# State space layer: the first sequence's halves of time in turn up to the softplus, gates and turned projections last

## The chip, the cores and the metric

One core of a Trainium2 chip runs the whole program. The metric is the device time of one execution in microseconds; for the kernel before it is the median of three runs. A trace of one further execution gives the start and end of every instruction on the engines: TensorE (PE, with PEld for its weight loads), VectorE (DVE), ScalarE (ACT), GpSimd (POOL), and the queues that issue transfers, SP's above all. Each engine works through its own queue in order.

## The reference, cut to what matters

The program is a network of eight layers on four sequences of 1024 steps with 128 features: attention, mixture of experts, gated attention, the mixture again, a state space layer, a gated feed-forward layer, a second attention and the feed-forward layer again. The change is inside the state space layer. Per sequence that layer computes:

```python
xn = (x - mu) / jnp.sqrt(var + EPS) * ln_gamma + ln_beta
xz = xn @ W_in.T
xs, z = jnp.split(xz, 2, axis=-1)            # 256 channels each
xc = conv over time of xs, 4 taps per channel, + conv_b
u = silu(xc)
proj = u @ W_xproj.T                          # 48 = 16 + 16 + 16 columns
dt_low, Bc, Cc = jnp.split(proj, [16, 32], axis=-1)
delta = softplus(dt_low @ W_dt.T + b_dt)
A = -jnp.exp(A_log)
for every step of time:                       # 16 states per channel
    h = exp(delta * A) * h + (delta * u) * B
    y = sum over states of h * C
y = (y + u * D) * silu(z)
return resid + y @ W_out.T
```

## The kernel before, in words

Channels lie on the partitions in two groups of 128 (g = 0, 1), time lies along the row in two halves of 512 (`HALVES`). The layer has two parts per sequence, both in `StateSpace.run`.

`prepare(b)` is a generator that makes what the scan of sequence b needs, a little with each step (`yield`). For b > 0 it first runs `turned_in(b)`: two normalisations (lines 1132 to 1150, statistics on VectorE, the scaling on ScalarE) and a transposition into `xt`. Then, in this order: the convolution as four matmuls per group and half with the taps folded into the input weights (line 1197), each followed by Silu into `u` (1203); the gates silu(z), one matmul (1210) and Silu into `gate` (1214) per group and half; the projection `proj`, two matmuls (1220) and a copy by ScalarE (1223) per half; the store of B's rows to device memory through SP's queue (`b_rows`, 1226); eight small transposes of `proj` (1229) and a copy (1231) into `by_time`, which holds C by time; then `delta` per group and half, one matmul (1239) and a `softplus`; last `du` = delta times u on VectorE (1247).

`softplus` (1100 to 1114) is max(x, 0) + log1p(exp(-|x|)), with log1p as a polynomial in factored form: on ScalarE Abs, Relu, Exp and four Squares, on VectorE four products of a chain (1113) and a last one into `delta` (1114). Its temporaries have one buffer each.

`scan(b, meanwhile)` loops over the 16 states n. Per state it reads row n of `b_rows` on all partitions (`bs`, SP's queue, 1254); per group ScalarE makes `decay` = exp(delta a) (1258), and VectorE makes the input `st` = du bs (1260) and scans along time in place (1261). Then TensorE turns the states (1267), ScalarE multiplies them with C into `hc` (1273), and TensorE adds them up in PSUM with an identity matmul (1274). Twice per state the scan takes one step of `meanwhile`, the preparation of the next sequence. After the 16 states the output is turned back (1289), u D is added (1293), the gate is multiplied (1296), and the output projection (1302) is added to the residual (1307).

The first sequence's preparation runs before any scan:

```python
for _ in prepare(0):
    pass
for b in range(B):
    scan(b, prepare(b + 1) if b + 1 < B else iter(()))
```

The pool `psum()` gives the preparation two PSUM buffers; `st` has four buffers, `decay` and `bs` two, `hc` three. The order of the instructions in an engine's queue is not quite that of the program: a scheduler places each by the buffers and inputs that it needs, so that instructions of the preparation and of the scan stand interleaved. It also puts a load of a function table in front of an activation whose function isn't in the table that ScalarE holds: Silu, Exp and Sqrt are in different ones; Abs, Relu, Copy, Identity and Square get by with any. The gather of the mixture layer before (line 796) ends just ahead of the first Silu, which waits for it because `u` takes memory that the mixture held.

Of the kernel before, what the change touches and what calls it, by code (L numbers as in the profile page):

```python
# [11 lines left out]
F32 = mybir.dt.float32  # L12
# [8 lines left out]
P = 128  # L21
B = 4
T = 1024
C = 128
NC = T // P
# [12 lines left out]
D_STATE = 16  # L38
D_CONV = 4
DT_RANK = 16  # L40
# [136 lines left out]
class Start:  # L177
# [8 lines left out]
    def steps(self, bank, pin):  # L186
        self.bank, self.pin = bank, pin
        while self.open:
            if next(self.gen) is False:
                self.open = False  # L190
            yield
# [863 lines left out]
class StateSpace(Begun):  # L1055
# [60 lines left out]
    def run(self, start):  # L1116
        k, tc, nc, NG = self.k, self.k.tc, self.k.nc, self.NG
        per = self.per
        PAD = D_CONV - 1
        NPROJ = DT_RANK + 2 * D_STATE  # L1120
        with ExitStack() as ctx:
            early = ctx.enter_context(tc.tile_pool(name="s_early", bufs=1))
            yield
            HALVES = [slice(0, 512), slice(512, 1024)]
# [3 lines left out]
            roots = early.tile([P, len(LOG1P[1])], F32, name="roots")  # L1128
# [23 lines left out]
            def turned_in(b):  # L1152

                xl = early.tile([P, NC, C], F32, tag="xl", name="xl")
                yield from normal(xl, k.xb(b))
                nc.vector.tensor_tensor(k.xb(b), k.xb(b), xl, ALU.add)
                xn = early.tile([P, NC, C], F32, tag="xn", name="xn")
                yield from normal(xn, xl)
                for h in range(2):
                    ps = start.bank()  # L1160
                    for c in range(4):
                        start.pin(nc.tensor.transpose(ps[:, c * P : (c + 1) * P], xn[:, h * 4 + c, :], k.ident))
                    nc.scalar.activation(
                        xt[:, PAD + h * 512 : PAD + (h + 1) * 512], ps, AF.Identity,
                        scale=self.ln[:, 0:1], bias=self.ln[:, 1:2],
                    )
                    yield
# [6 lines left out]
            one = ctx.enter_context(tc.tile_pool(name="s_one", bufs=1))  # L1174
            sb = ctx.enter_context(tc.tile_pool(name="s_sb", bufs=2))
            dram = ctx.enter_context(tc.tile_pool(name="s_dram", bufs=2, space=DRAM))
# [3 lines left out]
            ready = {}  # L1180

            def psum():
                return ps_t.tile([P, 512], F32, tag="pt", name="ps")
# [3 lines left out]
            def prepare(b):  # L1187

                if b:
                    yield from turned_in(b)  # L1190
                u = sb.tile([P, NG, T], F32, tag="u", name="u")
                gate = sb.tile([P, NG, T], F32, tag="gate", name="gate")
                for g in range(NG):
                    for h in range(2):
                        ps = psum()
                        for t in range(D_CONV):
                            nc.tensor.matmul(  # L1197
                                ps, taps[:, t, g * P : (g + 1) * P], xt[:, h * 512 + t : h * 512 + t + 512],
                                start=t == 0, stop=t == PAD,
                            )  # L1200
                            if t == 1:
                                yield
                        nc.scalar.activation(
                            u[:, g, HALVES[h]], ps, AF.Silu, bias=per[:, g, D_CONV : D_CONV + 1]
                        )
                        yield
                for g in range(NG):
                    for half in HALVES:
                        ps = psum()
                        nc.tensor.matmul(  # L1210
                            ps, self.w_in[:, (NG + g) * P : (NG + g + 1) * P],
                            xt[:, PAD + half.start : PAD + half.stop], start=True, stop=True,
                        )
                        nc.scalar.activation(gate[:, g, half], ps, AF.Silu)
                    yield
                proj = one.tile([NPROJ, T], F32, tag="proj", name="proj")
                for half in HALVES:
                    ps = psum()
                    for g in range(NG):
                        nc.tensor.matmul(  # L1220
                            ps[:NPROJ], self.w_x[:, g, :], u[:, g, half], start=g == 0, stop=g == NG - 1
                        )
                    nc.scalar.copy(proj[:, half], ps[:NPROJ])
                    yield
                b_rows = dram.tile([D_STATE, T], F32, tag="b_rows", name="b_rows")
                nc.sync.dma_start(b_rows, proj[DT_RANK : DT_RANK + D_STATE, :])
                ps = psum()[:, : NC * NPROJ].rearrange("p (c n) -> p c n", c=NC)
                for c in range(NC):
                    nc.tensor.transpose(ps[:, c, :], proj[:, c * P : (c + 1) * P], k.ident[:NPROJ, :NPROJ])
                by_time = sb.tile([P, NC, D_STATE], F32, tag="by_time", name="by_time")  # L1230
                nc.scalar.copy(by_time, ps[:, :, DT_RANK + D_STATE :])
                delta = sb.tile([P, NG, T], F32, tag="delta", name="delta")
                du = one.tile([P, NG, T], F32, tag="du", name="du")
                ready[b] = gate, u, b_rows, by_time, delta, du
                yield
                for g in range(NG):
                    for half in HALVES:
                        ps = psum()
                        nc.tensor.matmul(
                            ps, self.w_dt[:, g * P : (g + 1) * P], proj[:DT_RANK, half], start=True, stop=True  # L1240
                        )
                        yield from self.softplus(
                            delta[:, g, half], ps, per[:, g, D_CONV + 1 : D_CONV + 2], early, roots
                        )
                        yield
                for g in range(NG):
                    nc.vector.tensor_tensor(du[:, g, :], delta[:, g, :], u[:, g, :], ALU.mult)

# [60 lines left out]
# [4 lines that stand above are left out]
# [568 lines left out]
```

## Time and profile before

| what | value |
|---|---|
| median of three runs | 3334.68 us (3333.33 to 3335.18) |
| the profiled execution, its own time | 3334.47 us |
| its span, first to last instruction | 3332.7 us |
| busy: TensorE, VectorE, ScalarE | 2974.0, 2326.5, 1820.5 us |
| VectorE's scans (1261): count, mean | 128, 2.28 us |
| hc copies (1273): count, mean | 512, 0.48 us |
| table loads in the carrying scans (from 1892.5 to 2345): mean | 1.28 us |
| VectorE's waits in scan 0, 1 and 2 | 13.1, 18.6 and 19.7 us |

A line of a time line gives start, duration, engine, line and operation, output and inputs with their shapes, the count, and in brackets the idle time of the engine before it with what ended it. TensorE runs an f32 matmul in two passes, and the trace lists each pass: x8 are four matmuls. A line of the table by stage gives the stretch, its length, the busy time and count of instructions of each engine, the granted clock of TensorE as a share of full speed, and the transfers' share and rate. Consecutive lines of a stretch of a time line overlap slightly, since an engine begins the next instruction before the last has quite ended.

### The profile page before, as it was taken

Reading aid. Unit: us, or ns where it says so; the run is one execution under the profiler, and the core shown is the slowest. Engines: PE = TensorE matmul, PEld = TensorE weight load, DVE = VectorE, ACT = ScalarE, POOL = GpSimd, SP = SyncE. Lnnn points to the kernel's source line nnn. Section 1 sums busy time; section 2 is a strip of 40 time slices with the busy share of each in tenths; the row PEclk is TensorE's granted clock in tenths of the full one; section 3 lists DMA queues with packets and bytes.
Section 4 is the critical chain, followed back from the end, with each engine's and each line's share of the span. In section 5 each row is a group of like instructions: output and inputs, shape, how many; then the busy total and the mean of one; then the engine's idle time right before and its main releaser. Section 6 shows DMA issues by size and latency. Waiting matters only on the chain. (4 is left out here: it accounts for less than half of the span.)

```text
span 3332.7 us, 46103 instructions
## 1 busy us (share of the span) xinstructions
PE 2974.0 (89%) x16624; PEld 1699.2 (51%) x16624; DVE 2326.5 (70%) x5413; ACT 1820.5 (55%) x3822; POOL 289.4 (9%) x299
## 2 busy tenths in 40 slices
PE   7999999999999988699897597888778899999988
PEld 4555555555555566445565244444445444444435
DVE  5777777777777667575564589888976767676634
ACT  4555555556555432355332698989653365555662
POOL 3000000000000014410034000000002101010000
PEclk9999999999999999799899798999999799898999
DMA  3110000000000001100011111111202111121100
GB/s 108 43 34 15 16 17 15 17 16 15 17 16 15 15 15 39 54 0 0 1 35 45 43 58 57 58 51 55 66 26 57 29 42 50 31 50 30 31 2 26
DMA packets 84901, 109.39 MB, mean 33 GB/s; under 512 B 26048, under 2 KB 66544, under 8 KB 82240
## 3 DMA queue, kind: packets, MB, share of 16 engines
q1 hardware_dynamic: 59136, 69.50, 6.7%
q0 software_dynamic: 18688, 30.65, 3.6%
q10 hardware_dynamic: 6848, 6.29, 0.6%
q8 instruction: 130, 2.13, 0.3%
q14 instruction: 99, 0.81, 0.1%
HBM read 90.76 MB, written 15.60 MB: 32 GB/s over the span
## 5 line engine op out<-in xcount | busy, mean ns | idle before, releaser
L389 ACT ACTIVATE p<-p,tops 128x640 f32<-128x640 f32 (+7 forms) x512 | 392.2, 768 | 288.0 <-DVE tops L387 226.6
L380 DVE CUSTOM_DVE_ANT_0 p<-s,mask 128x512 f32<-128x512 f32 (+3 forms) x768 | 392.0, 551 | 130.2 <-PE s L374 129.4
L1632 ACT ACTIVATE p<-x 128x512 f32<-128x512 f32 (+3 forms) x768 | 337.6, 490 | 249.1 <-PE x L1631 179.5
L1571 DVE TENSOR_REDUCE tops<-s 128x2 f32<-128x1024 f32 (+3 forms) x384 | 361.2, 955 | 137.0 <-PE s L1567 96.5
L1274 PE MATMUL acc<-hc,ident 128*128 128x512 f32 x512 | 270.2, 652 | 92.4 <-ACT hc L1273 91.6
L374 PE MATMUL s<-kt,qt 64*128 64x512 f32 (+3 forms) x1536 | 311.3, 516 | 20.2 <-DVE tops L380 19.8
L482 PEld LDWEIGHTS t<-ident,p 128*128 128x128 f32 x2304 | 263.0, 141 | 80.8 <-issue 66.3
L1261 DVE TENSOR_TENSOR_SCAN st<-decay,st 128x1024 f32<-128x1024 f32 x128 | 288.8, 2278 | 10.9 <-ACT decay L1258 10.4
L497 PE MATMUL o<-pt,vv 128*64 128x256 f32 (+1 forms) x2560 | 291.1, 365 | 0.0
L482 PE MATMUL t<-ident,p 128*128 128x128 f32 x2304 | 283.7, 273 | 1.6 <-ACT p L389 1.6
L1626 PE MATMUL x<-q,k 75*128 75x512 bf16 (+3 forms) x768 | 224.0, 339 | 27.5 <-ACT p L1632 14.9
L1562 PE MATMUL s<-k,q 72*128 72x512 bf16 (+3 forms) x768 | 217.0, 349 | 27.5 <-DVE tops L1571 19.2
L488 ACT COPY pt<-t 128x512 f32<-128x512 f32 (+1 forms) x320 | 155.2, 495 | 156.9 <-DVE pt L490 148.8
L1273 ACT ACTIVATE hc<-ps,by_time 128x256 f32<-128x256 f32 x512 | 200.6, 478 | 47.6 <-PE ps L1267 47.5
L490 DVE COPY pt<-t 128x512 f32<-128x512 f32 x320 | 212.2, 684 | 16.5 <-PE t L482 16.3
L497 PEld LDWEIGHTS o<-pt,vv 128*64 128x64 f32 x2560 | 166.8, 136 | 96.7 <-issue 28.5
L374 PEld LDWEIGHTS s<-kt,qt 64*128 64x128 f32 x1536 | 124.5, 187 | 146.1 <-issue 77.9
L1274 PEld LDWEIGHTS acc<-hc,ident 128*128 128x128 f32 x512 | 91.7, 198 | 208.5 <-ACT hc L1273 190.0
L1260 DVE TENSOR_TENSOR st<-du,bs 128x1024 f32<-128x1024 f32 x128 | 151.8, 1216 | 47.0 <-PE ps L1267 46.8
L696 PE MATMUL acc<-d,xl 128*128 128x480 f32 (+1 forms) x384 | 155.5, 567 | 27.7 <-DVE d L691 27.7
L1267 PEld LDWEIGHTS ps<-ident,st 128*128 128x128 f32 x1024 | 126.3, 147 | 97.0 <-issue 61.3
L1660 PE MATMUL o<-p,vx 128*32 128x512 f32 (+3 forms) x1536 | 173.7, 525 | 0.0
(301 smaller groups left out, 4778.9 us busy)
## 6 DMA issues: line engine op xcount, KB each, us to landing
bs<-b_rows SPq DMA_DIRECT2D x64, 512.0 KB
share<-shares SPq DMA_DIRECT2D x256, 64.0 KB
k<-b_parts POOLq DMA_DIRECT2D x16, 576.0 KB, 12.5
q<-b_parts POOLq DMA_DIRECT2D x48, 192.0 KB, 11.8
shares<-rows SPq DMA_DIRECT2D x512, 0.5 KB
b_parts<-part SPq DMA_DIRECT2D x24, 256.0 KB
w_W<-in_W_dram ACTq DMA_DIRECT2D x16, 256.0 KB
y_rows<-y SPq DMA_DIRECT2D x16, 192.0 KB
```

What stands on the lines that cost most here:

```text
L374: pe(nc.tensor.matmul(s[:, h, : hi - lo], q[feats, ib * P : (ib + 1) * P], kk[feats, lo:hi], start=True, stop=True,))
L380: ve(nc.vector.tensor_tensor_reduce(p[:, h, i, lo:hi], s[:, h, : hi - lo], m, -1.0, 3.4e38, ALU.add, ALU.min, tops[:, h, i, at : at + 1],))
L389: exp = nc.scalar.activation(p[:, h, i, :width], p[:, h, i, :width], AF.Exp, bias=tops[:, h, i, 0:1], scale=-1.0, accum_out=sums[:, h, i : ...
L482: pe(nc.tensor.transpose(t[:, m, h, i * P : (i + 1) * P], p[:, h, i, jb * P : (jb + 1) * P], k.ident))
L490: nc.vector.tensor_copy(pt[:, :, lo:], t[:, m, :, lo:])
L497: pe(nc.tensor.matmul(o[feats, lo:], pairs[n]["v"][:, jb, feats], pt[:, h, lo:], start=jb == 0, stop=jb == (gq + 1) * Q - 1,))
L1261: nc.vector.tensor_tensor_scan(st, decay, st, 0.0, ALU.mult, ALU.add)
L1274: nc.tensor.matmul(acc[:, c : c + 2, :].rearrange("p c d -> p (c d)"), k.ident, hc.rearrange("p c d -> p (c d)"), start=n == 0, stop=n == ...
L1562: start.pin(nc.tensor.matmul(s[:, a, : hi - lo], qq[:ROWS, two + a, ib * P : (ib + 1) * P], kk[:ROWS, two + a, lo:hi], start=True, stop=ha ...
L1571: nc.vector.tensor_reduce(tops[:, half, two : two + 2, n], s[:, :, : hi - lo], AX.X, ALU.max)
L1626: start.pin(nc.tensor.matmul(x[:, lo:], kk[:FULL, a, jb * P : (jb + 1) * P], qq[:FULL, a, hq * 512 + lo : (hq + 1) * 512], start=True, sto ...
L1632: nc.scalar.activation(p[:, a, lo:], x[:, lo:], AF.Exp)
```

## The change

`prepare` gets two inner generators. `products(h)` makes both groups of `u` for one half of time and the projection of that half; `steps(h)` makes `delta` of one half. For the first sequence the order is products(0), steps(0), products(1), steps(1): the first half goes through softplus before the second half is begun. For the others it is products(0), products(1), steps(0), steps(1). In both, `b_rows` is stored behind products(1); the turned projections (`by_time`) and the gates come behind the last softplus, `du` after them. What is computed is the same, and so is the number of steps that `prepare` yields.

```diff
--- before.py
+++ after.py
@@ -1190,8 +1190,12 @@
                     yield from turned_in(b)
                 u = sb.tile([P, NG, T], F32, tag="u", name="u")
                 gate = sb.tile([P, NG, T], F32, tag="gate", name="gate")
-                for g in range(NG):
-                    for h in range(2):
+                proj = one.tile([NPROJ, T], F32, tag="proj", name="proj")
+                delta = sb.tile([P, NG, T], F32, tag="delta", name="delta")
+
+                def products(h):
+
+                    for g in range(NG):
                         ps = psum()
                         for t in range(D_CONV):
                             nc.tensor.matmul(
@@ -1204,6 +1208,44 @@
                             u[:, g, HALVES[h]], ps, AF.Silu, bias=per[:, g, D_CONV : D_CONV + 1]
                         )
                         yield
+                    ps = psum()
+                    for g in range(NG):
+                        nc.tensor.matmul(
+                            ps[:NPROJ], self.w_x[:, g, :], u[:, g, HALVES[h]], start=g == 0, stop=g == NG - 1
+                        )
+                    nc.scalar.copy(proj[:, HALVES[h]], ps[:NPROJ])
+                    yield
+
+                def steps(h):
+
+                    for g in range(NG):
+                        ps = psum()
+                        nc.tensor.matmul(
+                            ps, self.w_dt[:, g * P : (g + 1) * P], proj[:DT_RANK, HALVES[h]], start=True, stop=True
+                        )
+                        yield from self.softplus(
+                            delta[:, g, HALVES[h]], ps, per[:, g, D_CONV + 1 : D_CONV + 2], early, roots
+                        )
+                        yield
+
+                yield from products(0)
+
+                if b == 0:
+                    yield from steps(0)
+                yield from products(1)
+                b_rows = dram.tile([D_STATE, T], F32, tag="b_rows", name="b_rows")
+                nc.sync.dma_start(b_rows, proj[DT_RANK : DT_RANK + D_STATE, :])
+                if b:
+                    yield from steps(0)
+                yield from steps(1)
+                ps = psum()[:, : NC * NPROJ].rearrange("p (c n) -> p c n", c=NC)
+                for c in range(NC):
+                    nc.tensor.transpose(ps[:, c, :], proj[:, c * P : (c + 1) * P], k.ident[:NPROJ, :NPROJ])
+                by_time = sb.tile([P, NC, D_STATE], F32, tag="by_time", name="by_time")
+                nc.scalar.copy(by_time, ps[:, :, DT_RANK + D_STATE :])
+                du = one.tile([P, NG, T], F32, tag="du", name="du")
+                ready[b] = gate, u, b_rows, by_time, delta, du
+                yield
                 for g in range(NG):
                     for half in HALVES:
                         ps = psum()
@@ -1213,36 +1255,6 @@
                         )
                         nc.scalar.activation(gate[:, g, half], ps, AF.Silu)
                     yield
-                proj = one.tile([NPROJ, T], F32, tag="proj", name="proj")
-                for half in HALVES:
-                    ps = psum()
-                    for g in range(NG):
-                        nc.tensor.matmul(
-                            ps[:NPROJ], self.w_x[:, g, :], u[:, g, half], start=g == 0, stop=g == NG - 1
-                        )
-                    nc.scalar.copy(proj[:, half], ps[:NPROJ])
-                    yield
-                b_rows = dram.tile([D_STATE, T], F32, tag="b_rows", name="b_rows")
-                nc.sync.dma_start(b_rows, proj[DT_RANK : DT_RANK + D_STATE, :])
-                ps = psum()[:, : NC * NPROJ].rearrange("p (c n) -> p c n", c=NC)
-                for c in range(NC):
-                    nc.tensor.transpose(ps[:, c, :], proj[:, c * P : (c + 1) * P], k.ident[:NPROJ, :NPROJ])
-                by_time = sb.tile([P, NC, D_STATE], F32, tag="by_time", name="by_time")
-                nc.scalar.copy(by_time, ps[:, :, DT_RANK + D_STATE :])
-                delta = sb.tile([P, NG, T], F32, tag="delta", name="delta")
-                du = one.tile([P, NG, T], F32, tag="du", name="du")
-                ready[b] = gate, u, b_rows, by_time, delta, du
-                yield
-                for g in range(NG):
-                    for half in HALVES:
-                        ps = psum()
-                        nc.tensor.matmul(
-                            ps, self.w_dt[:, g * P : (g + 1) * P], proj[:DT_RANK, half], start=True, stop=True
-                        )
-                        yield from self.softplus(
-                            delta[:, g, half], ps, per[:, g, D_CONV + 1 : D_CONV + 2], early, roots
-                        )
-                        yield
                 for g in range(NG):
                     nc.vector.tensor_tensor(du[:, g, :], delta[:, g, :], u[:, g, :], ALU.mult)
```

## The prediction

> **What bounds the kernel now.** First the busy time of each engine by stage: the fill (the first sequence's preparation, nothing beside it) and the four scans, the first three of which carry the next sequence's preparation.
>
> ```profile
> core 0: us, PE busy (x) PEld busy (x) DVE busy (x) ACT busy (x) POOL busy (x), PEclk, DMA share, GB/s
> 1839.70:1892.50 52.80, 23.03 (x50) 8.37 (x51) 24.44 (x31) 33.59 (x53) 0.00 (x0) 0.66 0.09 32
> 1892.50:2041.20 148.70, 126.53 (x470) 67.15 (x470) 134.89 (x130) 133.68 (x239) 0.00 (x0) 0.94 0.18 61
> 2041.20:2193.40 152.20, 127.50 (x504) 71.10 (x504) 134.18 (x135) 132.48 (x237) 0.00 (x0) 0.96 0.17 56
> 2193.40:2345.00 151.60, 127.99 (x485) 69.50 (x486) 129.88 (x142) 129.63 (x224) 0.00 (x0) 0.93 0.16 53
> ```
>
> In the fill no engine is full: it is a chain. In the scans three engines are near 90%, so the mean says little; what counts is where VectorE waits. Then the order of time in the fill:
>
> ```profile
> 1839.70 1.28 ACT L1203 ACT_TABLE_LOAD   x1 [25.11 <-DVE x L796]
> ...
> 1841.73 9.14 PE L1197 MATMUL ps<-xt,w_taps 128*128 128x512 f32 x16 [18.20 <-ACT u L1203]
> ...
> 1860.36 0.69 ACT L1106 ACTIVATE tmp<-ps,w_channels 128x512 f32<-128x512 f32 x1 [0.78 <-PE ps L1239]
> ...
> 1861.64 1.28 ACT L1108 ACT_TABLE_LOAD   x1
> ...
> 1862.94 0.63 ACT L1108 ACTIVATE tmp<-tmp 128x512 f32<-128x512 f32 x1
> ...
> 1868.14 2.07 PE L1239 MATMUL ps<-proj,w_wdtT 16*128 16x512 f32 x2 [5.34 <-ACT delta L1107]
> ...
> 1890.16 4.46 DVE L1261 TENSOR_TENSOR_SCAN st<-decay,st 128x1024 f32<-128x1024 f32 x2
> ```
>
> The start (1839.70) is set by the mixture's gather and can't move. ScalarE then waits for TensorE until 1860.36; its work until then is the first two u by 1842.3, two more (1.4), four gates (2.4), two proj copies (1.2), by_time (0.3): of 18.1 us it idles 12.9. The four softplus run after that, and the second channel group's first scan ends at 1892.4. The fill has two table loads (Silu, then Exp).
>
> Last, VectorE's waits. Those over 2 us that fall between the last u activation and the end of the first softplus's scans:
>
> ```profile
> 1960.98 1.23 DVE L1260 TENSOR_TENSOR st<-du,bs 128x1024 f32<-128x1024 f32 x1 [3.71 <-PE ps L1267]
> ```
> ```profile
> 2103.78 2.36 DVE L1260 TENSOR_TENSOR st<-du,bs 128x1024 f32<-128x1024 f32 x2 [3.37 <-PE ps L1267]
> ...
> 2112.40 1.23 DVE L1260 TENSOR_TENSOR st<-du,bs 128x1024 f32<-128x1024 f32 x1 [4.06 <-PE ps L1267]
> ```
> ```profile
> 2256.97 1.22 DVE L1260 TENSOR_TENSOR st<-du,bs 128x1024 f32<-128x1024 f32 x1 [4.62 <-PE ps L1267]
> ...
> 2264.81 1.23 DVE L1260 TENSOR_TENSOR st<-du,bs 128x1024 f32<-128x1024 f32 x1 [3.31 <-PE ps L1267]
> ...
> 2271.96 6.66 DVE L1261 TENSOR_TENSOR_SCAN st<-decay,st 128x1024 f32<-128x1024 f32 x3 [2.42 <-ACT decay L1258]
> ```
>
> A product st waits for a state buffer that TensorE's transposes free, and these wait for ScalarE. What ScalarE does then is seen in its own time line (scan 0):
>
> ```profile
> 1955.04 1.28 ACT L1214 ACT_TABLE_LOAD   x1
> 1956.33 1.09 ACT L1214 ACTIVATE gate<-ps 128x512 f32<-128x512 f32 x2
> ...
> 1959.38 1.28 ACT L1258 ACT_TABLE_LOAD   x1
> ```
>
> So each carrying scan has two halves. Up to softplus, ScalarE (u, gates and their table loads) and TensorE (taps, gates, proj) set the pace and VectorE waits; from softplus on, VectorE (6.7 us a state, from two products at 1.13 and two scans at 2.2, plus 3.5 to 3.8 a softplus block) sets it and waits for almost nothing (at most 1.1 us in one place) until the scan's end.
>
> **Part 1, the fill.** No arithmetic is added or removed; the order is, and with it the table loads. In the built order of instructions ScalarE's loads in the fill go from 2 to 10: the scheduler puts Silu (u, gates) between the Exp of the softplus blocks. Eight more at 1.28 us (row L1108) are 10.3 us, against 12.9 of idle time that may be filled. I walk ScalarE's queue in its built order, with steps from the fill's rows: u 0.65, Abs 0.6, Relu 0.7, Exp 0.7, square 0.7, gate 0.6, load 1.28; a TensorE pass (two to a matmul) 0.85 with the clock at half, 0.43 at full, its result 1.2 or 0.6 after the last start.
> - Two u end at 1842.3 as before. proj (four slow passes from 1841.73) is ready at 1845.4, copied by 1846.0; dt (2.07, row L1239) gives Abs at 1848.1.
> - Abs, Relu, load, Exp, three squares: 1853.65. Load, u, fourth square: 1856.2.
> - Abs, Relu, load, Exp, load, u: 1861.5.
> - Two squares, proj copy, two squares: 1864.7.
> - Abs, Relu, load, Exp, by_time, two squares, load, gate, two squares, gate: 1873.2.
> - The fourth block with two loads and two gates: 1881.6. VectorE then has a product, delta (1883.1), du (1884.3), the first scan, which now stands behind this (1886.6), two products (1888.8), the second group's scan: 1891.0.
>
> That is 1.4 before the old 1892.4. But before, ScalarE's normalising (L1147) and VectorE's statistics stood partly in gaps of the fill; now they follow. The third state's products start at 1899.9 instead of 1900.5: -0.6. This has TensorE at full clock after dt. At half clock, the second tap group is 2.1 late for its u, proj 1.0, dt and a gate 0.9 each: +4.9, so +4.3. The page "TensorE: Matmul & The Clock Gate" (Part 1) lets the clock fall only after an idle window of about 3.4 us; the new gaps are up to 3.2, so by it the term is -0.6. The trace differs: the granted clock was 1.00 in 1861 to 1862, 0.93 in the next microsecond and 0.50 in 1863 to 1864, right behind the last pass at 1862.8. I go by the row, half-way: **+1.5**, ends -0.6 and +4.3.
>
> A rule against the change: "ScalarE: Activation LUTs" (What ACT_TABLE_LOAD costs) adds a drain of 1.38 to each load, 2.66 a switch. The rows show none: Relu ends at 1861.6, the load starts at 1861.64, Exp at 1862.94. By the page the fill is 8 x 1.38 = 11.0 worse and four further loads in the scans up to 5.5: the sum below would be about +7. I take the row.
>
> The b_rows store now waits for the second proj copy (1863.4, was 1858.8) and SP's bs reads behind it: with the old 2.1 to the first issue and 5 us in which the trace moves both, they land by 1870.6; the first product needs them at 1873.7. Cover 3 us, cost nothing.
>
> **Part 2, the three carrying scans.** The scan takes two steps of the preparation a state. Softplus stood behind 13 steps (8 taps, 2 gates, 2 proj, 1), now behind 10: 1.5 states sooner, and the gates come last. I walk the queues of the three engines in their built order, with the scan's rows (hc copies of half a state 1.43, decay 1.05, a softplus's seven activations 4.2), from the end of the hc copies behind the fourth u (1950.5 in scan 0, 2101.4 in scan 1, 2254.7 in scan 2):
> - Old order, scan 0: gates, loads and proj follow. VectorE's next six scans (states 8 to 10) end 26.5 later (1976.9), with waits of 3.7 and 0.3 on the way.
> - New order: load, decay, proj copy, hc, decay, Abs, Relu, Exp, hc, squares. The same scans end at 28.0, but six softplus products and one delta (4.9) stand among them, work that the old order still had ahead. From there on VectorE sets the pace in both. Gain 4.9 - 1.5 = 3.4.
> - In front of this point TensorE has two proj matmuls more (1.7 us; TensorE 97% busy here): scan 0 keeps **-1.7**.
> - Scan 1: same walk, 27.3 against 26.5 with 3.4 done, and the old waits of 1.1 and 0.2 at the first softplus go too: 3.9, less 0.9 for the part of proj that a smoother row of taps doesn't absorb: **-3.0**.
> - Scan 2: the old order piled gates, proj, by_time and dt into one stretch (waits 4.6, 3.3, 2.4, 1.9); scans that ended at 2287.2 end at 2283.0 with 3.4 of softplus done: 7.6, less 1.1: **-6.5**.
>
> The gates themselves cost 4 loads and 4 activations, 7.3 to 7.5 us of ScalarE a scan (2 loads more than before in scans 0 and 1, none in scan 2: the 4 above). Their cover is VectorE. Walked from the decay of state 12: ScalarE has decay 26 ready at 14.7, VectorE asks at 17.2; decay 28 at 23.5, asked at 23.8; one state buffer 0.4 late. So they are hidden, but with 0.3 us to spare at the last. Behind a late decay would stand VectorE's scan, and behind it du and the next sequence's products. The b_rows store of the next sequence moves two places up SP's queue of bs reads in scan 0 (between those of states 9 and 10), one in the others; it waits for a copy at state 6 or 7, so no read queues behind it for long. xt is read by the gates until late, and is written again only in the next scan. Everything after the last scan is in the same order on all queues.
>
> **Sum.** +1.5 - 1.7 - 3.0 - 6.5 = **-9.7** on the profiled execution's 3334.47 (span 3332.7, 1.8 around it): 3324.8; the median of the runs is 0.2 above that: **3325**. A measurement of this kernel can't tell less than about 0.2%, 6.7 us, from nothing.
>
> **The rivals.**
> - A, the waits vanish altogether: all of VectorE's waits behind the fourth u (4.3, 8.8, 12.3: 25.4) and a fill at -0.6: 3309. For it: VectorE is full from there on. Against it: proj is now in the crowded half.
> - B, waits only move: proj and dt in front take what the gates gave, scans give nothing, fill +1.5: 3336. For it: ScalarE and TensorE are both above 96% in that half, and the same 8 loads for u remain.
> - C, slower: the gates' loads are not covered. VectorE's queue has four softplus products and a delta in a row just there; if ScalarE isn't ahead, each scan pays up to 7.3 us: +21.9 - 9.7, 3347. It decides from 5.5 us a scan on (slower by 6.7). For it: the reserve of 0.3. Against it: ScalarE idles for VectorE's squares now (8.4 us over the three scans).
>
> **How the numbers follow.** The forecast 0.54 (its own range 3318 to 3332, the clock's two ends and 3 us of error in the walks), A 0.10, B 0.19, C 0.17. 3328.0 and 3341.4 are the bounds. Faster: A, and four fifths of the forecast: 0.54. Same: the rest of it, most of B: 0.27. Slower: C with a tail of B: 0.19. The range leaves out a third of A and C's worse half: 3312 to 3343.
>
> **What would show it.** Right: 10 loads in the fill, scan's second-group start near 1891 to 1895, each softplus's first product two states sooner, carrying scans of 147, 149 and 145 us, no VectorE wait over 2 us behind the fourth u. Wrong: a fill over 57 us; VectorE waits on decay at states 13 and 14 beside gate loads; a gap behind each load; a scan no shorter although softplus came sooner.

## The result, and the profile after

The changed kernel takes 3347.5 us (median of 5 runs, 3344.6 to 3354.4) where the kernel before takes 3334.7 (5 runs beside it, 3331.4 to 3336.8): a ratio of 1.0046, 95% interval 1.0035 to 1.0058. It is slower, by 12.8 us; the forecast was 3325, and the range ended at 3343. The profiled execution took 3347.5 us, its span is 3345.8.

First the busy time by stage, of the kernel after, with the same columns as before (stretch, its length, busy time and count of instructions of each engine, granted clock of TensorE, transfers):

```profile
core 0: us, PE busy (x) PEld busy (x) DVE busy (x) ACT busy (x) POOL busy (x), PEclk, DMA share, GB/s
1839.70:1892.50 52.80, 29.57 (x56) 9.99 (x56) 26.02 (x30) 44.58 (x64) 0.00 (x0) 0.66 0.09 32
1892.50:2048.00 155.50, 128.01 (x466) 66.33 (x466) 134.70 (x135) 136.44 (x240) 0.00 (x0) 0.94 0.17 58
2048.00:2209.60 161.60, 134.48 (x504) 71.14 (x504) 134.63 (x134) 135.55 (x236) 0.00 (x0) 0.93 0.16 53
2209.60:2362.00 152.40, 127.85 (x482) 68.25 (x482) 128.63 (x137) 127.81 (x219) 0.00 (x0) 0.93 0.16 53
```

ScalarE is busier in the fill by 11.0 us, about the eight further loads. The first two carrying scans took 155.5 and 161.6 us, 6.8 and 9.4 more than before, while VectorE's busy time is within 0.5 us of what it was (134.9 and 134.2); the third took 152.4, 0.8 more. So VectorE waits, and the question is where.

**The measure used from here on.** The layer begins with the first u activation and ends, for this purpose, at the first line of VectorE that adds u D for the last sequence (1293 before, 1305 after). In the profiled execution of before that stretch is 1840.99 to 2473.54, 632.6 us; of after 1841.15 to 2491.44, 650.3: +17.7. What lies outside it is the same program in both, 2700.2 and 2695.5 us; in the executions profiled below it was 2690 to 2716, with no pattern that follows the edits. The stretch is therefore the sharper instrument of the two, and each experiment is given with both. It is taken from one execution of each kernel. How well it repeats is seen in its last part, in which nothing is carried: from the end of the third scan to that line of VectorE it took 136.7 to 138.3 us in all kernels but after_st6 and late_silu, whose edits reach into it. So differences of 1 or 2 us are not read as effects.

Within a scan I add up the idle times in brackets on VectorE's lines, from the scan's begin (in scan 0, from the first scan line of the second channel group) to the end of state 10's second scan ("front": u, proj and the first softplus fall here), and from there to the first scan line of the next sequence ("rear": the other softplus blocks, and in the kernel after the gates). The seams differ a little from those of the table ahead of the prediction; the sum for before is the same within 0.1.

| VectorE's waits, us | front: scan 0, 1, 2 | sum | rear: scan 0, 1, 2 | sum |
|---|---|---|---|---|
| before | 13.1, 16.1, 20.9 | 50.2 | 0.0, 1.3, 0.0 | 1.3 |
| after | 10.6, 15.7, 13.0 | 39.3 | 9.2, 10.6, 10.0 | 29.8 |

The front gained 10.9, where the forecast's three terms make 11.2. The rear, which the forecast gave nothing, lost 28.5. The difference, +17.6, is the stretch's +17.7 almost by itself. (Two of the expectations below have 30.1 for the rear of after: that takes in a wait of 0.27 us at the first line that adds u D.) Here is the rear of scan 0 in the time line of VectorE, kernel after:

```profile
2002.06 0.69 DVE L1114 SCALAR_TENSOR_TENSOR delta<-tmp,delta 128x512 f32<-128x512 f32 x1
2004.76 1.22 DVE L1272 TENSOR_TENSOR st<-du,bs 128x1024 f32<-128x1024 f32 x1 [2.00 <-PE ps L1279]
2005.90 2.28 DVE L1273 TENSOR_TENSOR_SCAN st<-decay,st 128x1024 f32<-128x1024 f32 x1
2008.10 1.20 DVE L1272 TENSOR_TENSOR st<-du,bs 128x1024 f32<-128x1024 f32 x1
2009.22 2.28 DVE L1273 TENSOR_TENSOR_SCAN st<-decay,st 128x1024 f32<-128x1024 f32 x1
2018.40 1.22 DVE L1272 TENSOR_TENSOR st<-du,bs 128x1024 f32<-128x1024 f32 x1 [6.91 <-PE ps L1279]
2019.55 2.28 DVE L1273 TENSOR_TENSOR_SCAN st<-decay,st 128x1024 f32<-128x1024 f32 x1
```

Read it by states. The two scans (1273) at 2005.90 and 2009.22 are those of state 13. The products (1272) at 2004.76 and 2008.10 belong to state **14**: the scheduler has set each in front of a scan of the state before. With four state buffers the next product, at 2018.40, the first of state 15, takes the buffer of state 13's first group. TensorE turns the two groups of a state in alternation, so this buffer is free only when nearly all of state 13 has been turned, and the second group was scanned an instruction ago. The product waits 6.91 us for it. TensorE shows the chain in that time (one line is one group; x8 are eight transposes):

```profile
2011.55 0.87 PE L1279 MATMUL ps<-ident,st 128*128 128x128 f32 x6 [2.81 <-DVE st L1273]
2013.09 3.78 PE L1286 MATMUL acc<-hc,ident 128*128 128x512 f32 x4 [0.66 <-ACT hc L1285]
2016.67 1.91 PE L1279 MATMUL ps<-ident,st 128*128 128x128 f32 x8
```

It had waited 2.81 for that very scan; then come transposes, the hc copies (ScalarE, 2012.20), the sum, the last transposes, and at 2018.4 the buffer is free. And ScalarE, in the same stretch, has the gates and their loads:

```profile
2008.11 1.28 ACT L1256 ACT_TABLE_LOAD   x1
2009.40 0.60 ACT L1256 ACTIVATE gate<-ps 128x512 f32<-128x512 f32 x1
2012.20 1.57 ACT L1285 ACTIVATE hc<-ps,by_time 128x256 f32<-128x256 f32 x4 [2.20 <-PE ps L1279]
2013.64 0.61 ACT L1256 ACTIVATE gate<-ps 128x512 f32<-128x512 f32 x1
2014.27 1.28 ACT L1270 ACT_TABLE_LOAD   x1
```

In before, VectorE's line at the same states has softplus work between almost any two steps, and no wait. The product of state 14 stands behind both scans of state 13, and that of state 15 (the last line here) comes 11 us after them:

```profile
2001.53 2.29 DVE L1261 TENSOR_TENSOR_SCAN st<-decay,st 128x1024 f32<-128x1024 f32 x1
2003.74 1.46 DVE L1113 SCALAR_TENSOR_TENSOR tmp<-tmp 128x512 f32<-128x512 f32 x2
2005.12 1.22 DVE L1260 TENSOR_TENSOR st<-du,bs 128x1024 f32<-128x1024 f32 x1
2006.25 0.69 DVE L1113 SCALAR_TENSOR_TENSOR tmp<-tmp 128x512 f32<-128x512 f32 x1
2006.86 2.28 DVE L1261 TENSOR_TENSOR_SCAN st<-decay,st 128x1024 f32<-128x1024 f32 x1
...
2013.58 1.46 DVE L1113 SCALAR_TENSOR_TENSOR tmp<-tmp 128x512 f32<-128x512 f32 x2
2014.95 1.22 DVE L1260 TENSOR_TENSOR st<-du,bs 128x1024 f32<-128x1024 f32 x1
```

In after, the same wait stands at 2180.39 in scan 1 (6.76) and at 2340.46 in scan 2 (6.07).

### The profile page after: what moved, and what is told of

Its sections match the earlier page's. It is cut to its first block, busy times and chain, and to the rows that moved or that the text cites. A ratio compares the mean times of both kernels' runs of the same rounds, so it can differ in the third digit from the quotient of the medians.

```text
span 3345.8 us, 46082 instructions
## 1 busy us (share of the span) xinstructions
PE 2985.0 (89%) x16624; PEld 1698.3 (51%) x16624; DVE 2328.6 (70%) x5413; ACT 1836.9 (55%) x3834; POOL 289.7 (9%) x299
## 5 line engine op out<-in xcount | busy, mean ns | idle before, releaser
L1574 PE MATMUL s<-k,q 72*128 72x512 bf16 (+3 forms) x768 | 217.9, 350 | 24.8 <-DVE tops L1583 17.2
L490 DVE COPY pt<-t 128x512 f32<-128x512 f32 x320 | 212.2, 684 | 17.2 <-PE t L482 17.1
L1279 PE MATMUL ps<-ident,st 128*128 128x128 f32 x1024 | 145.8, 285 | 41.6 <-DVE st L1273 41.6
```

The lines of the kernel that those rows point to most:

```text
L1279: nc.tensor.transpose(ps[:, m, g * P : (g + 1) * P], states[g][:, (c + m) * P : (c + m + 1) * P], k.ident,)
L1574: start.pin(nc.tensor.matmul(s[:, a, : hi - lo], qq[:ROWS, two + a, ib * P : (ib + 1) * P], kk[:ROWS, two + a, lo:hi], start=True, stop=ha ...
```

## The experiments

Two theories. **LOADS**: the gates' four loads and activations (7.3 us a scan) make decays and hc copies late, whatever VectorE's order is. **ORDER**: it is VectorE's queue, which the scheduler has built with a state's products in front of the scans of the state before.

### Which part: the fill or the scans

The kernel fill_only has the new order in the first sequence and the old one in the others:

```diff
+                if b == 0:
                     proj = one.tile([NPROJ, T], F32, tag="proj", name="proj")
...
+                else:
+                    for g in range(NG):
+                        for h in range(2):
+                            ps = psum()
+                            for t in range(D_CONV):
...
```

> The first sequence in the new order, the other three prepared in the old one; nothing is left out. Both theories of the loss (below) put it into the three carrying scans, so here only the fill's gain of 1.2 us is left: 3333 to 3334, VectorE's waits in the scans as before (13, 19, 20 us). If the fill's ten table loads cost something that the start of the scan hides, it is over 3336.

Measured: 3333.9 us, ratio 1.0001 (0.9991 to 1.0011); stretch 632.4, waits front 48.9, rear 3.0. The fill neither brings nor costs anything that can be measured; the loss is in the later sequences.

### The loads away, or the order away

gates_noload leaves the function out of the later sequences' gates, so that no load goes with them:

```diff
-                        nc.scalar.activation(gate[:, g, half], ps, AF.Silu)
+                        nc.scalar.activation(gate[:, g, half], ps, AF.Identity if b else AF.Silu)
```

> The changed kernel with the gates of sequences 1 to 3 computed by Identity in place of Silu, which leaves the Silu of the gates out of the result and needs no table; everything else is the same, in the same place. Table loads in the carrying scans go from 15, 15 and 16 to 11, 11 and 13. LOADS: 3329 to 3333 (4 loads, 5.1 us, a scan). ORDER: the built queue of VectorE loses the products in front of the scans too, so 3328 to 3336; this run bounds what the loads and what hangs on them cost, and doesn't part the two.

after_pinned keeps the gates and their loads, and ties VectorE's order: the first product of a state is placed behind the last scan of the state before, in the queue only, with no semaphore.

```diff
+                        product = nc.vector.tensor_tensor(st, du[:, g, :], bs, ALU.mult)
+                        if scanned is not None and g == 0:
+                            tc.add_manual_dep(
+                                product.ins, scanned.ins.name,
+                                mybir.DependencyInfo(mybir.DependencyClass.NoSync, mybir.DependencyReason.DATA),
+                                reason="order",
+                            )
+                        scanned = nc.vector.tensor_tensor_scan(st, decay, st, 0.0, ALU.mult, ALU.add)
```

> The changed kernel with one order added on VectorE's queue and no wait: the first product of a state stands behind the last scan of the state before. Theory ORDER (the loss is that VectorE's queue puts a state's products in front of the scans of the state before, so that behind softplus a product waits for the transposes of what was scanned just now): the waits of 6.9 and 6.8 us go, 3330 to 3337. Theory LOADS (the gates' four table loads and four activations, 7.3 us of ScalarE a scan, hold up decays and hc copies whatever VectorE's order): 3344 to 3350, with waits on decay in place of those on transposes.

Measured: gates_noload 3328.4, ratio 0.9985 (0.9974 to 0.9996), stretch 629.0; after_pinned 3327.2, ratio 0.9987 (0.9978 to 0.9996), stretch 632.1. Each alone takes the loss away. The first doesn't tell the theories apart, since without the loads the scheduler no longer sets products ahead at the end of scan 0; both products of state 14 stand behind the last scan of state 13:

```profile
2006.14 2.28 DVE L1273 TENSOR_TENSOR_SCAN st<-decay,st 128x1024 f32<-128x1024 f32 x1
2008.34 2.34 DVE L1272 TENSOR_TENSOR st<-du,bs 128x1024 f32<-128x1024 f32 x2
```

The second does: all of the gates' loads are there, and 18.2 us are gone, 10.6 of them in the rear. (The program is faster than ORDER's 3330 to 3337 had it, since the front lost 9.1 us of waits too, which neither theory had.) VectorE in the same place, after_pinned, and ScalarE's loads and decays beside it:

```profile
1997.78 0.69 DVE L1114 SCALAR_TENSOR_TENSOR delta<-tmp,delta 128x512 f32<-128x512 f32 x1
2001.34 2.29 DVE L1280 TENSOR_TENSOR_SCAN st<-decay,st 128x1024 f32<-128x1024 f32 x1 [2.87 <-ACT decay L1271]
2003.83 2.29 DVE L1280 TENSOR_TENSOR_SCAN st<-decay,st 128x1024 f32<-128x1024 f32 x1 [0.20 <-ACT decay L1271]
2006.04 2.33 DVE L1273 TENSOR_TENSOR st<-du,bs 128x1024 f32<-128x1024 f32 x2
2011.37 2.29 DVE L1280 TENSOR_TENSOR_SCAN st<-decay,st 128x1024 f32<-128x1024 f32 x1 [3.00 <-ACT decay L1271]
```
```profile
1998.87 1.28 ACT L1271 ACT_TABLE_LOAD   x1
2000.16 1.15 ACT L1271 ACTIVATE decay<-delta,a 128x1024 f32<-128x1024 f32 x1
...
2008.90 1.28 ACT L1271 ACT_TABLE_LOAD   x1
2010.19 1.15 ACT L1271 ACTIVATE decay<-delta,a 128x1024 f32<-128x1024 f32 x1
```

What is left are two waits of 2.87 and 3.00 for a decay, each behind a load: LOADS as such, 6 us a scan. So LOADS in its strong form (the order is of no account) falls, but the loads aren't hidden either.

### The order alone

noload_ahead has no loads at the gates, and forces the products of 14 and 15 in front of the scans of 13 and 14, by the same kind of tie:

```diff
+                        early_product = n in (13, 14) and b + 1 < B
+                        if early_product:
+                            product(n + 1, g)
                         scanned = nc.vector.tensor_tensor_scan(st, decay, st, 0.0, ALU.mult, ALU.add)
+                        if early_product:
+                            tc.add_manual_dep(
+                                scanned.ins, made[n + 1, g][1].ins.name,
...
```

> The kernel after with Identity in place of Silu in the gates of the later sequences (the gates are left out of the function, so that no table load goes with them), and with VectorE's queue forced at the end of each carrying scan: the products of states 14 and 15 stand in front of the scans of states 13 and 14. The kernel with Identity alone took 3328.4. ORDER: the product of state 15 waits again for the transposes of state 13, 4 to 7 us in each of the three scans, although no load is there: 3338 to 3349. LOADS: without the loads nothing is late, the order of two products is of no account: 3325 to 3332.

In this set of runs the kernel before itself took 3349.3, so ratios and stretches are read, not times. Measured: ratio 1.0005 (0.9992 to 1.0018), stretch 634.9, 5.9 more than without the forced order. ORDER's wait came back bare in scan 2, with no load near:

```profile
2336.89 1.23 DVE L1273 TENSOR_TENSOR st<-du,bs 128x1024 f32<-128x1024 f32 x1 [6.28 <-PE ps L1298]
```

In scans 0 and 1 the scheduler filled the same gap with statistics of a later normalisation (in scan 0 4.9 us of them between a scan that ends at 2021.06 and the product at 2025.98). In scan 1 the product of state 15 still waited 1.33. The mechanism is as ORDER has it, but the 4 to 7 us in each scan (12 to 21 in all) are a miss: the ratio lies between the ranges of the two theories, and only one gap of three stayed empty.

noload_pinned has neither the loads nor the order:

> The kernel after with Identity for Silu in the later gates (the function is left out) and with the tie (first product of a state behind the last scan of the state before). VectorE's waits in the three carrying scans, up to the second scan of state 10 and behind it: before 50.2 and 1.3, after 39.3 and 30.1, tied 30.2 and 19.2, without the loads 38.4 and 8.6. If the tie's 9 us in the first half and the loads' 21 in the second are separate things, the sum is here about 30 and 8: stretch 617 to 623. If both are the same lateness in two places, nothing is added: 627 to 631.

Measured: 3328.0, ratio 0.9987 (0.9977 to 0.9996), stretch 629.0, the same as without the loads alone. Without late decays there is nothing for the tie to mend. With it the rear's waits make a table of four:

| rear waits, us | products ahead | tied |
|---|---|---|
| gates' loads there | 29.8 (after) | 19.2 (after_pinned) |
| no loads | 16.2 (noload_ahead) | 8.4 (noload_pinned) |

Above the 8.4 the loads cost 10.8, the order 7.8, and both together 21.4. The waits at the product of state 15 itself are 0, 1.33 and 6.28 in noload_ahead, 7.6 together, which agrees with the difference of the sums. The forced order isn't quite that of the kernel after, and two of its gaps were filled, so 7.8 is probably less than the order costs there.

### Controls: the tie, the buffers, the gates' place

before_pinned is the kernel before with the same tie:

> Control: the kernel before with the same tie (first product of a state behind the last scan of the state before), whose queue has hardly any product to move. If the tie by itself brings time, 3320 to 3328, and the 3327 of the tied kernel after is no merit of the halves. If it only mends what the change disturbed (ORDER), 3329 to 3336. LOADS says nothing of it.

Ratio 1.001 (0.9999 to 1.0021), stretch 635.9, 3.4 more than before: the tie brings nothing by itself.

after_st6 has six state buffers in place of four:

```diff
-                        st = sb.tile([P, T], F32, tag="st", name="st", bufs=4)
+                        st = sb.tile([P, T], F32, tag="st", name="st", bufs=6)
```

> The kernel after with six state buffers for four. ORDER: the product of state 15 then waits for the transposes of state 12, long done, so VectorE's waits of 6 to 7 us near the end of each carrying scan go and nothing else does: 3324 to 3336. LOADS: decays and hc copies are late whatever the buffers, VectorE waits for decay in place of PSUM: 3341 to 3349.

Ratio 1.0004 (0.9986 to 1.0023), stretch 634.9 (15.4 less than after), rear 14.6. By the ratio this is some 3334 us where before takes 3333, in ORDER's range and outside that of LOADS. The first product of state 15, which waited 6.91, waits 1.93:

```profile
2020.76 0.69 DVE L1114 SCALAR_TENSOR_TENSOR delta<-tmp,delta 128x512 f32<-128x512 f32 x1
2023.38 1.23 DVE L1272 TENSOR_TENSOR st<-du,bs 128x1024 f32<-128x1024 f32 x1 [1.93 <-PE ps L1279]
```

So the long wait was for the state buffer, as the releaser said, and not for the decay. Shorter waits stay, 14.6 us of them in the rear.

gates_last is the kernel before with one edit: in the later sequences the gates come behind the last softplus, and the halves stay as they were.

```diff
...
+                if b:
+                    yield from gates()
                 for g in range(NG):
                     nc.vector.tensor_tensor(du[:, g, :], delta[:, g, :], u[:, g, :], ALU.mult)
```

> The kernel before with one edit: in the later sequences the gates stand behind the last softplus; the halves of time and the first sequence stay as they were. Its queue of VectorE has at the end of a scan the same pairs (scan of 13, product of 15, scan of 14, product of 15) as the kernel after. If the gates' place alone makes the loss, by ORDER or by LOADS: 3340 to 3352, with waits of 4 us and more for PSUM at state 15. If the turned halves are needed for it: 3329 to 3337.

Ratio 1.0062 (1.0037 to 1.0086, four runs), by which it would take some 3354 where before takes 3333, just above the expected range; stretch 659.5; front 39.5, rear 35.8. Its VectorE at state 15:

```profile
2030.15 4.47 DVE L1268 TENSOR_TENSOR_SCAN st<-decay,st 128x1024 f32<-128x1024 f32 x2 [1.71 <-ACT decay L1265]
2041.24 1.23 DVE L1267 TENSOR_TENSOR st<-du,bs 128x1024 f32<-128x1024 f32 x1 [6.62 <-PE ps L1274]
```

The gates' place alone makes the loss, and also the front's whole gain (39.5 against 39.3): what relieves the front is that the gates have left it. The rest of the change, halves and fill, is worth 9.2 us of stretch on top of that.

### Where else the gates could go

gates_with_u puts the gates of each half behind its u, where Silu's table is loaded anyway:

```diff
+                    if b:
+                        for g in range(NG):
+                            ps = psum()
+                            half = HALVES[h]
...
+                            nc.scalar.activation(gate[:, g, half], ps, AF.Silu)
+                        yield
                     ps = psum()
```

> The changed kernel with the gates of sequences 1 to 3 taken out from behind softplus and put into each half of the products, right behind that half's u and ahead of proj; complete. No gate stands in VectorE's half, and softplus starts half a state later than in the changed kernel. ORDER and LOADS both: the waits of 6 to 7 us go; if the first half's gain of some 3 us a scan stays, 3324 to 3330; if the gates in front cost what they cost before, 3331 to 3336.

A miss: 3346.1, ratio 1.0047 (1.003 to 1.0065), stretch 644.5. The rear is mended (7.7), but the front is at 53.1, above even the kernel before, with this line in scan 0 and one of the same length in scan 1:

```profile
1963.16 2.36 DVE L1283 TENSOR_TENSOR st<-du,bs 128x1024 f32<-128x1024 f32 x2 [5.58 <-PE ps L1290]
```

ScalarE loads tables at 1948.75, 1950.75, 1954.67, 1957.16, 1961.07 and 1964.93 there. One gate follows a u on the same table; for the other the scheduler put a decay between, so that it has a pair of loads of its own, in the half where ScalarE has no room.

after_four makes all four gates in one step and keeps decays from between them, so that two loads of a scan's four go; `behind` places one instruction behind another in its queue. pinned_four adds the tie of products and scans.

```diff
-                        nc.scalar.activation(gate[:, g, half], ps, AF.Silu)
-                    yield
+                        made = nc.scalar.activation(gate[:, g, half], ps, AF.Silu)
+                        if b and g == 0 and half.start == 0:
+                            behind(made, last[0])
+                        last[1] = made if b else None
+                yield
+                yield
...
+                def ordered(made):
+                    if last[1] is not None:
+                        behind(made, last[1])
+                    last[:] = made, None
...
+                        ordered(nc.scalar.activation(decay, delta[:, g, :], AF.Exp, scale=self.a[:, g, n : n + 1]))
```

> The kernel after, with the four gates of a later sequence in one step and no decay among them on ScalarE (the first gate stands behind the last decay issued, the next decay behind the last gate): two table loads for the gates of a scan in place of four. By this VectorE's queue also loses the product of state 15 right behind the second scan of 13. Measured by the stretch from the first u of the layer to the last gate multiplication (before 632.6, after 650.3, tied 632.1, without the gates' loads 629.0). ORDER: the PSUM wait of 6 to 7 us is gone, and what the tied kernel still waited for decay (5.9 a scan) shrinks by half or more: 623 to 630, the whole program 3322 to 3331 where before takes 3333. LOADS: only the two loads of each scan are saved, 3 x 2.6: 640 to 645, the program 3338 to 3342.

> The same with the tie too (the first product of a state stands behind the last scan of the state before). ORDER: with the gates in one stretch there is little left for the tie to mend: within 2 us of the kernel without it, stretch 623 to 631. LOADS: as without the tie, 640 to 645.

after_four: 3331.8, ratio 0.9998 (0.999 to 1.0006), stretch 633.1, rear 14.3. The long wait is gone and 17.2 us with it, as ORDER had it, but the rest didn't shrink as expected (623 to 630): state 13's decays now come behind all four gates. pinned_four: 3344.0, ratio 1.003 (1.0022 to 1.0038), stretch 643.9, a miss for ORDER. The number lies where LOADS had it, but LOADS had after_four there as well, which it isn't. Scan 1 alone has 27.5 us of waits, 18.8 of them in the front, far from the gates. Why the tie costs there is not explained.

late_silu computes everything with no load for the gates at the scan's end: the gate is copied there, and gets its Silu a scan later behind a u.

```diff
-                        nc.scalar.activation(gate[:, g, half], ps, AF.Silu)
+                        nc.scalar.activation(gate[:, g, half], ps, AF.Identity if b else AF.Silu)
...
+                        if h == 0 and b > 1:
+                            behind(silu(b - 1, g), made)
...
```

> A kernel that computes everything and has no table load for the gates of a later sequence: at the end of a scan the gates are only copied (Identity, any table will do), and Silu is put on them one scan later, right behind a u activation that has loaded Silu's table (the last sequence's in its own scan, two activations of 128x1024 with two pairs of loads of their own). The stretch from first u to the last gate multiplication was 632.6 before, 650.3 after, 629.0 without the function. ORDER and LOADS agree that the waits near the end of a scan are those of the kernel without the function (8.6 in all, after 30.1); two activations of about 1 us each more in the half where ScalarE is full cost 0 to 2.5 a scan: 627 to 635, the program 3326 to 3335 where before takes 3333.

Stretch 631.1, front 40.2, rear 6.3: in the layer as expected, 19.2 us shorter than after and 1.4 shorter than before. The program took 3336.8, ratio 1.001 (1.0001 to 1.002), just outside what was expected; its profiled execution spent 2708 us outside the layer, 8 more than that of before. That part isn't touched by the edit, and the runs don't say why it is longer.

## Why the prediction was wrong

- **The fill** (+1.5, ends -0.6 and +4.3): a little better than its better end. The third state's products start at 1899.29, where 1900.5 was the old time: -1.2. The better end assumed TensorE at full clock behind dt: the granted clock was 0.50 from 1849 to 1852, 1.00 from 1853 to 1865 and 0.50 again from 1866 on, so the second tap group (3.70 us), proj and dt had the full clock and the gates half of it. In fill_only, though, the stretch is only 0.2 shorter than in before, so the fill's gain doesn't show by itself. There are ten loads, and the activation behind a load starts 1.29 us after the load's start, which decides for the row and against the further drain of 1.38 us that the Trainium skill gives ("ScalarE: Activation LUTs", What ACT_TABLE_LOAD costs):

```profile
1848.60 1.28 ACT L1108 ACT_TABLE_LOAD   x1
1849.89 0.63 ACT L1108 ACTIVATE tmp<-tmp 128x512 f32<-128x512 f32 x1
...
1899.29 2.32 DVE L1272 TENSOR_TENSOR st<-du,bs 128x1024 f32<-128x1024 f32 x2
```

- **The front of the scans** (-1.7, -3.0, -6.5): right in sum: by VectorE's waits -2.5, -0.4 and -7.9, -10.9 together before rounding, where -11.2 was forecast. Scan 1 gave 2.6 less, scan 2 1.4 more, so the agreement of the sum is in part luck. In scan 0 the walk's end was 28.0 behind the hc copies of the fourth u; it was 27.5 (1950.49 to 1978.00).
- **The gates' cover: the step that failed.** Part 2 put the cost of the gates' loads behind softplus at nothing: "one state buffer 0.4 late. So they are hidden". Its text asks for the decays of states 13 and 14 and for that one buffer; the buffer of state 15 isn't in it. The first late buffer cost 2.0 (2004.76), and the one of state 15 6.91: in VectorE's queue the second scan of 13 stood behind a product of 14 that was itself late, and the product of 15 right behind that scan, so that it paid for transposes, hc copies and sum of a whole state. Cost of the term: 0 forecast, 28.5 measured.
- **Rival C** named the place and nearly the size: up to 7.3 a scan, 3347; it was 9.5 a scan. Its cause is half of it, and its sign, waits on decay at states 13 and 14, didn't come: both long waits are for transposes, and waits of 3 us on decay show in this place only with the tie. There the loads by themselves make 3 us twice a scan; the order that the scheduler chose beside them, or the two together, does the rest.
- **The sum.** By the stretch, -1.2 - 10.9 + 28.5 = +16.4 of the +17.7. The profiled execution as a whole moved by 13.0 (the medians by 12.8), as the rest of the program was 4.7 shorter in that of after than in that of before.

What stays open: the 8.4 us of rear waits without loads and with the tie (before had 1.3) weren't followed up; 6.7 of them stand at three products that wait for transposes, at 2139.19 and 2151.14 in scan 1 and at 2307.60 in scan 2, at least 25 us ahead of the scan's end. Nor was it found why the tie also takes 9.1 us out of the front (30.2 against 39.3, 9.9 to 10.3 in each scan), which it doesn't do without the gates' loads (38.5).

No version beat the kernel before in the layer by more than 1.4 us with all its work done. after_pinned is faster than both as a program, than before by 0.04 to 0.22%, but its stretch is only 0.5 us shorter than that of before, so this gain is not put down to the change.

## What to carry to other kernels

When a scheduler orders the queues, walk the queue of the engine that sets the pace in its built order up to the last instruction, and for each instruction that takes a buffer ask which instruction frees it and how far ahead that stands: a product one place behind the scan whose buffer it needs pays the whole chain over three engines. Work moved out of a full stretch into another needs reserve there: here a decay behind a block of load, activations and load came 3 us late even in the better order. A reserve of 0.3 us in a walk is none. And where the program outside the change scatters by as much as the effect, measure the stretch that the change can reach.

## What the runs showed of the hardware

TensorE's clock fell within the 6.91 us wait, and work in the wait took longer for it. By the granted clock in steps of one microsecond, kernel after:

```profile
2011.00:2012.00 1.00, 0.45 (x4) 0.45 (x5) 0.50 (x1) 0.00 (x0) 0.00 (x0) 1.00 0.83 266
2012.00:2013.00 1.00, 0.43 (x4) 0.19 (x2) 0.00 (x0) 0.80 (x3) 0.00 (x0) 0.73 0.12 49
2013.00:2014.00 1.00, 0.91 (x1) 0.50 (x2) 0.00 (x0) 1.00 (x4) 0.00 (x0) 0.50 0.00 0
...
2019.00:2020.00 1.00, 1.00 (x3) 0.46 (x3) 1.00 (x2) 1.00 (x3) 0.00 (x0) 0.86 0.03 8
```

The last figure but two is the clock. The 0.73 puts its fall at about 2012.5, when the engine had been idle for 2.81 us (to 2011.55) and had then worked for 0.87; it came back within 2019 to 2020. Meanwhile the sum took 3.78 in place of the 1.98 of the one at 2001.97, and the eight transposes 1.91 in place of 1.04 at 2003.79: by these durations an estimated 2.7 of the 6.91. In the waits of scans 1 and 2 the clock was 0.50 too (from 2173 to 2179 and from 2337 to 2340). So a wait of VectorE that leaves TensorE idle for some 3 us can lengthen itself. The idle stretch is shorter than the window of about 3.4 us that the Trainium skill gives ("TensorE: Matmul & The Clock Gate", Part 1), and the measurement decides here.
